# cv1 by one step of Strassen's scheme in six of eight images, its additions in the second attention, and four changes of VectorE's order in attention

## The chip, the cores and the metric

The kernel runs on one core of a Trainium2 chip. What counts is the device time of one execution, in microseconds (us). An execution has five engines that run side by side and wait for each other through semaphores: TensorE (PE in the profile, its weight loads PEld), VectorE (DVE), ScalarE (ACT), GpSimd (POOL) and the sync engine (SP), whose queue issues most of the transfers from and to DRAM. Matmuls write to PSUM, everything else that stays on the core lives in SBUF.

## What is computed

For x of 8 images with 512 channels and 32 x 32 points, all in float32 (`cbs` is convolution, batch norm with fixed statistics, silu):

```python
def layer(x):                                  # called as x + layer(group_norm(x))
    t = cbs(x, cv1_w, cv1_bn, 0)               # 1x1, 512 -> 512 channels
    ys = [t[:, :256], t[:, 256:]]
    for i in range(2):
        yi = ys[-1]
        z = cbs(yi, m_cv1_w[i], m_cv1_bn[i], 1)             # 3x3, 256 -> 256
        z = bot_attention(z, m_qkv_w[i], m_rw[i], m_rh[i])  # 4 heads of 64, 1024 points
        z = silu(bn_eval(conv2d(z, m_cv2_w[i], 0), m_cv2_bn[i]))
        ys.append(yi + z)
    return cbs(concatenate(ys, axis=1), cv2_w, cv2_bn, 0)   # 1x1, 1024 -> 512
```

The attention is softmax(q (k + r) / 8) v with r = rw + rh, for each head over all 1024 points.

## The kernel before

An image is 1024 columns (two halves of 512) by 512 channels (four blocks of 128 partitions). The loop over images is unrolled (`for b in range(B)`, line 1129). For each image: conv3x3 of the first bottleneck (a Winograd form; its transformed input is made by `tiles_in`, line 346, its transformed weights `u` are loaded from DRAM), the first attention, the 1x1 convolution `m2` (line 894), conv3x3 of the second bottleneck, the second attention, `m2`, and cv2. Work of the next image is laid between: cv1 of image b+1 is computed at the end of image b's first attention.

`cv1` (line 857) goes by blocks of 128 output channels: 4 blocks of input channels times 2 halves, 8 matmuls of 128x128 by 512 columns a block, into one PSUM tile of two banks; two silus on ACT take it to y0 (first 256 channels) or into y1, a padded image. Two blocks (y1) are put before and after the last sums of the attention (`first`, `second`, lines 1192 and 1200), two (y0) behind `m2` (line 1214).

cv2 and the q, k, v projection already use one step of Strassen's scheme in Winograd's form (7 products of half-size blocks in place of 8, with four sums of weights and four sums of inputs): `strassen` (line 940), `project_strassen` (line 537). The sums of weights are made once, in image 0 (`make_ws`, `make_sq`), and kept in DRAM.

`attention_fast` (line 637) goes through four groups (channel block c, half), each of four pairs of 128-row tiles. For a pair: `logits` puts 16 matmuls in a PSUM tile for each tile of the pair, ACT takes the exponential (L666), DVE adds it to `acc` (L672 for the first pair of a group, L674 for the others); `times_v` multiplies the pair before by v into `av_ps` (L688), one PSUM tile with a single buffer. When a group is through, ACT copies half of it (L695) and DVE adds the other half (L696), which frees the tile. The sums of a group go over PE (`sums`), to DRAM and back, through a reciprocal (`spread`, L750), and out again as the broadcast tile `rs`; `scale` (L762) multiplies with it. The last group takes a short way (`last_sums`, L724; L796, a reciprocal over 512 elements, L797). What is to be done beside the attention is in the table `behind`: its entry g is called after the first pair of group g, an entry (g, p) after pair p of group g, entries 4 and 5 at the end, before and after `last_sums`.

Order: each engine works through its instructions in a fixed order that the framework's scheduler chooses from priorities (the order in which they are written) and readiness in its own model. `tc.issue_after(ins)` holds the instructions of a block, on the engine of `ins`, behind `ins`. Tiles with one `tag` share its `bufs` buffers: the tag "u" has five buffers of 1 MB for all large weights (u, w1, w2, ws, sq), "x" four, "xr" two, and in PSUM `ps_big` has three tiles of two banks.

Lines that the prediction names: cv1's matmuls L343; the products of cv2's scheme L934; m2's matmuls L900; group norm L443 (bn_stats) and L477 (apply), called step by step from `ahead` through `norm`.

Of the kernel before, what the change touches and what calls it, by code (L numbers as in the profile page):

```python
# [44 lines left out]
F32 = mybir.dt.float32  # L45
I32 = mybir.dt.int32
AF = mybir.ActivationFunctionType
# [14 lines left out]
def kernel(  # L62
# [260 lines left out]
    def stages(act, small, ps_big, ps_av, n_pt):  # L323


        def silu(dst, src, k):

            return nc.scalar.activation(dst, src, AF.Silu, scale=sh[:, k : k + 1], bias=bh[:, k : k + 1])  # L328

        def table_of(func):  # L330

            nc.scalar.activation(spare, zero, func)

        def conv1x1(w_of, rhs_of, nk, ks=None, ps=None, ends=None, by_half=False):

# [201 lines left out]
        def project_strassen(n, z, sq, mid):  # L537
# [35 lines left out]
            def add_r(c, half, src=None):  # L573
                dst = img(kr[:, c, ts(half, HALF)])
                rw = rw_sb[:, n, c, :].unsqueeze(1).to_broadcast([P, ROWS, F])
                rh = rh_sb[:, n, c, ts(half, ROWS)].unsqueeze(2).to_broadcast([P, ROWS, F])
                tt(dst, dst if src is None else img(src), rw, ALU.add)
                tt(dst, dst, rh, ALU.add)

            t = act.tile([P, 4, HALF], F32, tag="pt", name="t_z", bufs=n_pt)  # L580
            t1, t2, t3, t4 = (t[:, i] for i in range(4))
# [55 lines left out]
        def attention_fast(n, z, at, behind, sq=None, mid=None):  # L637
# [13 lines left out]
            def logits(pair):  # L651
                g, j0 = pair[0]
                c, half = groups[g]
                pt = act.tile([P, PAIR, 2, HALF], F32, tag="pt", name="pt", bufs=n_pt)
                pts[pair[0]] = pt
                for i, (_, j) in enumerate(pair):
                    ps = ps_big.tile([P, 2, HALF], F32, tag="big", name="l_ps")
                    for hd in range(2):
                        r = slice(hd * HD, (hd + 1) * HD)
                        for kh in range(2):  # L660
                            o = j * P + kh * HD
                            nc.tensor.matmul(  # L662
                                ps[kh * HD : (kh + 1) * HD, hd, :], kr[r, c, o : o + HD],
                                q[r, c, ts(half, HALF)], start=True, stop=True,
                            )
                    exp = nc.scalar.activation(pt[:, i], ps, AF.Exp, scale=SCALE)  # L666
                if pair is pairs[-1]:
                    with tc.issue_after(exp.ins):
                        table_of(AF.Silu)
                if j0 == 0:  # L670
                    accs[g] = act.tile([P, 2, HALF], F32, tag="acc", name="acc", bufs=2)
                    return nc.vector.tensor_tensor(accs[g], pt[:, 0], pt[:, 1], ALU.add)  # L672
                for i in range(PAIR):
                    ins = nc.vector.tensor_tensor(accs[g], accs[g], pt[:, i], ALU.add)  # L674
                return ins

            def times_v(pair):
                g, j0 = pair[0]
                c, half = groups[g]
                pt = pts.pop(pair[0])  # L680
                if j0 == 0:
                    avs[g] = ps_av.tile([P, 2, HALF], F32, tag="av", name="av_ps")
                for i, (_, j) in enumerate(pair):
                    for kh in range(2):
                        r = slice(kh * HD, (kh + 1) * HD)
                        for hd in range(2):
                            o = c * P + hd * HD
                            nc.tensor.matmul(  # L688
                                avs[g][hd * HD : (hd + 1) * HD, kh, :], vT[r, j, o : o + HD],
                                pt[r, i, hd, :], start=(j == 0), stop=(j == NJ - 1),  # L690
                            )
                if j0 + PAIR == NJ:
                    av = avs.pop(g)
                    dst = ao[:, c, ts(half, HALF)]
                    nc.scalar.copy(dst, av[:, 0])  # L695
                    nc.vector.tensor_tensor(dst, av[:, 1], dst, ALU.add)  # L696

            def sums(g):

# [65 lines left out]


            NQ = NJ // PAIR
            s_drams, rss = {}, {}
# [171 lines left out]
        def strassen(b, ws, y0, y1):  # L940
# [85 lines left out]

            return part1, part2, part3

        def cv2_part(w2, ys, oc, ks=range(2 * NM)):
# [99 lines left out]
    for b in range(B):  # L1129
# [36 lines left out]


        parts = {}


        norm = s.group_norm(xs) if more else iter(())
        groups = iter(range(NM * NH))

        def ahead():
            nonlocal w1
            g = next(groups)
            if g > 0:
                next(norm, None)
            if g == 0:
                w1 = load_w1() if more else load_w2(1)  # L1180
                if b > 0:
                    for at in ((0, 0), (0, 1), (0, 2), (1, 0)):
                        us[at] = load_u(1, *at)
            if b == 0:
                if g == 0:
                    raws[1, 1, 0], raws[1, 1, 1] = load_raws_y0(1, 1)
                    make(1, 1, [2])
                    del us[1, 2]
                elif g <= NM:
                    make(1, 1, [0], [g - 1])  # L1190

        def first():
            nonlocal nxt
# [19 lines left out]
        if more:  # L1213
            s.cv1(w1, xs, nxt, y1n, Y0S)
        else:
            parts[3] = s.cv2_part(w1, (y0, y1), 3)
            parts[0] = s.cv2_part(w1, (y0, y1), 0, range(NM))
# [148 lines left out]
```

## Time and profile before

| | |
|---|---|
| median of 3 runs | 2366.81 us (2366.19 to 2371.23) |
| profiled execution | 2367.23 us, of which the span of its instructions 2365.4 us |
| granted TensorE clock, mean | 0.997 of full speed |
| PE av_ps L688, 4096 records | 487.8 us busy |
| PE l_ps L662, 4096 records | 486.1 us busy |
| PE conv3x3 L879, x u, 2720 records | 306.9 us busy |
| PE cv1, x w, L343, 512 records | 227.1 us busy |
| DVE acc L674, 384 | 469.5 us busy |
| ACT exp L666, 512 | 494.9 us busy |
| transfers | 226.39 MB, mean 96 GB/s |

A float32 matmul appears as two records in the profile. A record's mean time (600 ns for 512 columns) is longer than the distance at which records follow each other, since they are pipelined; the rate is read from how many stand in a stretch. In the tables a group's row ends with the idle time of its engine in front of it and the engine, tile and line that ended most of that time. From one image to the next (images 2 to 6) the same point of the program returns every 288.8 us.

### The profile page before, as it was taken

How to read it: one execution, taken by the hardware profiler on the slowest of the kernel's cores; microseconds unless marked ns; L12 is line 12 of the kernel's file. 1: busy time of each engine (PE TensorE's matmuls, PEld its weight loads, DVE VectorE, ACT ScalarE, POOL GpSimd, SP SyncE). 2: the span in 40 equal slices, each digit the busy share in tenths (PEclk: the TensorE clock that was granted, in tenths of full speed). 3: DMA queues.
4: the chain of work that ended last, by engine and by line, in shares of the span. 5: the costliest groups of instructions: out<-in, count | busy, mean ns of one | idle time of the engine just before them, and what ended most of it. 6: DMA issues, size and time to landing. Idle time of an engine off the chain costs nothing.

```text
span 2365.4 us, 36291 instructions
## 1 busy us (share of the span) xinstructions
PE 2321.6 (98%) x14794; PEld 1181.0 (50%) x14794; DVE 1751.7 (74%) x2811; ACT 944.5 (40%) x1246; POOL 87.9 (4%) x305
## 2 busy tenths in 40 slices
PE   7999999999999999999999999999999999999998
PEld 4536346363553635536364463645536364463643
DVE  8866777677786877868678675886767867677674
ACT  1442524435244351544425344253433525335352
POOL 1000000000100001000010000100001000000001
PEclk9999999999999999999999999999999999999999
DMA  7412225030340304303052031611207021160202
GB/s 251 152 53 89 91 90 213 16 129 15 123 176 15 130 15 164 140 10 130 23 208 89 29 112 33 248 42 54 86 28 263 29 85 55 42 221 15 85 10 69
DMA packets 93069, 226.39 MB, mean 96 GB/s; under 512 B 27872, under 2 KB 49312, under 8 KB 80224
## 3 DMA queue, kind: packets, MB, share of 16 engines
q1 hardware_dynamic: 81376, 174.71, 21.8%
q0 software_dynamic: 11520, 49.29, 5.3%
q8 instruction: 118, 1.93, 0.3%
q14 instruction: 55, 0.45, 0.1%
HBM read 190.41 MB, written 33.55 MB: 95 GB/s over the span
## 4 chain that ended last, share of the span: by engine, by line
PE 89%; DVE 6%; DMA 2%; ACT 2%; issue 1%; SPq 0%; POOL 0%; DVEq 0%; ACTq 0%
PE av_ps L688 16%; PE l_ps L662 15%; PE c_ps L879 14%; PE ps L343 12%; PE c L934 8%; PE p_ps L556 7%; PE c_new L934 6%; PE m_ps L900 5%; PE pv_ps L560 3%; DVE acc L674 2%; ACT pt L666 1%; PE p_ps L560 1%; DVE acc L672 1%; PE s_ps L724 1%; DMA rs<-r_dram 1%; PE s_ps L706 1%
## 5 line engine op out<-in xcount | busy, mean ns | idle before, releaser
L666 ACT ACTIVATE pt<-l_ps 128x1024 f32<-128x1024 f32 x512 | 494.9, 1023 | 425.0 <-PE l_ps L662 423.6
L674 DVE TENSOR_TENSOR acc<-acc,pt 128x1024 f32<-128x1024 f32 x384 | 469.5, 1223 | 84.9 <-ACT pt L666 60.1
L688 PE MATMUL av_ps<-pt,vT 64*64 64x512 f32 x4096 | 487.8, 593 | 10.7 <-DVE ao L696 10.7
L662 PE MATMUL l_ps<-q,kr 64*64 64x512 f32 x4096 | 486.1, 591 | 0.9
L879 PEld LDWEIGHTS c_ps<-v_in,u 128*128 128x128 f32 x2720 | 306.3, 192 | 7.9 <-issue 6.7
L879 PE MATMUL c_ps<-v_in,u 128*128 128x128 f32 x2720 | 306.9, 275 | 1.1 <-DVE v_in L400 1.1
L688 PEld LDWEIGHTS av_ps<-pt,vT 64*64 64x64 f32 x4096 | 157.1, 133 | 284.0 <-issue 216.7
L662 PEld LDWEIGHTS l_ps<-q,kr 64*64 64x64 f32 x4096 | 158.2, 133 | 269.6 <-issue 255.4
L343 PE MATMUL ps<-x,w 128*128 128x512 f32 x512 | 227.1, 600 | 2.2 <-DVE x L477 2.2
L343 PEld LDWEIGHTS ps<-x,w 128*128 128x128 f32 x512 | 97.0, 192 | 130.3 <-issue 127.2
L407 ACT COPY m<-c_ps 128x256 f32<-128x256 f32 x96 | 35.4, 369 | 224.9 <-PE c_ps L879 219.8
L934 PE MATMUL c_new<-t_in,ws 128*128 128x512 f32 x288 | 124.6, 592 | 0.0
L672 DVE TENSOR_TENSOR acc<-pt 128x1024 f32<-128x1024 f32 x64 | 78.3, 1223 | 58.0 <-ACT pt L666 58.0
L900 PE MATMUL m_ps<-ao,m_sb 128*128 128x512 f32 x256 | 112.5, 592 | 0.0
L762 DVE TENSOR_TENSOR ao<-ao,rs 128x512 f32<-128x512 f32 x64 | 44.1, 689 | 65.8 <-DMA rs<-r_dram 65.1
L328 ACT ACTIVATE m_kept<-m_kept,bh,sh 128x512 f32<-128x512 f32 x42 | 31.9, 806 | 146.0 <-DVE m_kept L1018 86.3
L934 PEld LDWEIGHTS c_new<-t_in,ws 128*128 128x128 f32 x288 | 54.8, 190 | 68.8 <-issue 66.0
L328 ACT ACTIVATE t<-m_ps,bh,sh 128x512 f32<-128x512 f32 x64 | 48.0, 775 | 83.9 <-PE m_ps L900 82.5
L556 PE MATMUL p_ps<-t_z,sq 128*128 128x512 f32 x168 | 81.3, 593 | 0.0
L372 POOL MEMSET w_rows<- 128x16 f32 x96 | 12.2, 127 | 1805.6 <-PE s_ps L706 1111.8
L900 PEld LDWEIGHTS m_ps<-ao,m_sb 128*128 128x128 f32 x256 | 48.7, 190 | 61.2 <-issue 61.2
L328 ACT ACTIVATE z<-z,bh,sh 128x512 f32<-128x512 f32 x64 | 48.6, 806 | 50.9 <-DVE z L436 50.9
(223 smaller groups left out, 2704.9 us busy)
## 6 DMA issues: line engine op xcount, KB each, us to landing
u<-u SPq DMA_DIRECT2D x85, 1024.0 KB
x<-in_x_dram SPq DMA_DIRECT2D x32, 512.0 KB
x_res<-in_x_dram POOLq DMA_DIRECT2D x28, 512.0 KB, 8.1
out_dram<-m_kept POOLq DMA_DIRECT2D x28, 512.0 KB, 7.5
w<-in_cv_w_dram SPq DMA_DIRECT2D x13, 1024.0 KB
u<-u_new POOLq DMA_DIRECT2D x12, 1024.0 KB, 5.8
rs<-r_dram SPq DMA_DIRECT2D x96, 128.0 KB
ws<-s SPq DMA_DIRECT2D x24, 512.0 KB
```

Source lines behind the costliest of these rows:

```text
L328: return nc.scalar.activation(dst, src, AF.Silu, scale=sh[:, k : k + 1], bias=bh[:, k : k + 1])
L343: nc.tensor.matmul(ps[:, half, :], w_of(k), rhs_of(k, half), start=(k == begin), stop=(k == end))
L556: nc.tensor.matmul(ps[:, o, :], w[:, o, :], rhs, start=not onto, stop=True, skip_group_check=onto)
L560: nc.tensor.matmul(v[:, ts(j, P)], rhs[:, ts(j, P)], w[:, 2, :], start=j == 0 and not onto, stop=True, skip_group_check=True,)
L662: nc.tensor.matmul(ps[kh * HD : (kh + 1) * HD, hd, :], kr[r, c, o : o + HD], q[r, c, ts(half, HALF)], start=True, stop=True,)
L666: exp = nc.scalar.activation(pt[:, i], ps, AF.Exp, scale=SCALE)
L672: return nc.vector.tensor_tensor(accs[g], pt[:, 0], pt[:, 1], ALU.add)
L674: ins = nc.vector.tensor_tensor(accs[g], accs[g], pt[:, i], ALU.add)
L688: nc.tensor.matmul(avs[g][hd * HD : (hd + 1) * HD, kh, :], vT[r, j, o : o + HD], pt[r, i, hd, :], start=(j == 0), stop=(j == NJ - 1),)
L879: nc.tensor.matmul(ps[:, row, col, :], us[i][:, k, row, SLOT[col], :], vs[i][:, k, row, col, :], start=(k == 0), stop=(k == NM - 1),)
L900: nc.tensor.matmul(pss[oc][:, half, :], m2_sb[:, n, k, ts(oc, P)], ao[:, k, ts(half, HALF)], start=(k == 0), stop=(k == NM - 1),)
L934: nc.tensor.matmul(ps[:, o, :], w[:, k, ts(o, P)], rhs[part][:, c, :], start=(k == 0 and not onto), stop=(k == KB - 1), skip_group_check=onto,
```

## The change

A new function `strassen_cv1` computes cv1 of images 2 to 7 (during images 1 to 6). Its weight sums are made in image 0's second attention (`make_sw`) and loaded with w1 (`load_sw`). Before the last sums of the first attention stand two products and eight additions of 128x512 for t1 to t4 (`begin`), after them a third product onto the first one's PSUM tile and its two silus (`go_on`), behind `m2` the other four (`rest`). Results wait unfinished in y0, y1 and spare tiles; six additions of 128x1024 in the second attention (`add_y0`, `add_y1`) and six silus at its end (`finish`) complete them.

In attention: add_r of the second half in the projection goes ahead of v and q; where the projection is `project_strassen`, the first addition to acc of group 1 is held behind L696; `scale` of a group goes one pair later; in image 0 the steps of the group norm begin one group earlier and make_sq moves. The loads of u for the second conv3x3 go ahead of w1, and the one for its second half of output channels, `load_u(1, 1, 0)`, is no longer made ahead.

```diff
+    sw_dram = tc.dram_tile([P, 4, NX // 2, C], F32, name="sw")
+
+    def make_sw():
+        halves = []
+        for o in range(2):
+            a = act.tile([P, NX, C], F32, tag="x", name="w1_half", bufs=NX)
+            nc.sync.dma_start(a, cv1_w[:, ts(o, C)].rearrange("(k p) o -> p k o", p=P))
+            halves.append((a[:, : NX // 2], a[:, NX // 2 :]))
+        (a11, a12), (a21, a22) = halves
+        parts = [act.tile([P, 2, NX // 2, C], F32, tag="xr", name="sw_new", bufs=2) for _ in range(2)]
+        s1, s2, s3, s4 = (t[:, j] for t in parts for j in range(2))
+        nc.vector.tensor_tensor(s1, a21, a22, ALU.add)
+        nc.vector.tensor_tensor(s2, s1, a11, ALU.subtract)
+        nc.vector.tensor_tensor(s3, a11, a21, ALU.subtract)
+        nc.vector.tensor_tensor(s4, a12, s2, ALU.subtract)
+        for h, t in enumerate(parts):
+            nc.gpsimd.dma_start(sw_dram[:, 2 * h : 2 * h + 2], t)
+
+    def load_sw():
+        w = ring([P, 4, NX // 2, C], "sw")
+        nc.sync.dma_start(w, sw_dram)
+        return w
...
             with tc.issue_after(last.ins):
                 tt(k1, k1, u[:, 1], ALU.add)
-                add_r(0, 1)
+                last = add_r(0, 1)
+            with tc.issue_after(last.ins):
                 tt(v1, v1, v_of(u[:, 2]), ALU.add)
                 tt(q1, q1, u[:, 0], ALU.add)
...
                     with tc.issue_after(exp.ins):
-                        table_of(AF.Silu)
+                        silu_in.append(table_of(AF.Silu))
+                if j0 == 0 and g == 1 and later is not None:
+                    accs[g] = None
+                    return exp
+                return add_up(pair)
+
+            def add_up(pair):
+                g, j0 = pair[0]
+                pt = pts[pair[0]]
                 if j0 == 0:
                     accs[g] = act.tile([P, 2, HALF], F32, tag="acc", name="acc", bufs=2)
                     return nc.vector.tensor_tensor(accs[g], pt[:, 0], pt[:, 1], ALU.add)
...
-                        if at_q == 0 and g > 1:
+                        if at_q == 1 and g > 1:
                             scale(g - 2, rss.pop(g - 2))
...
                     times_v(pairs[i - 1])
+                    if i < len(pairs) and accs.get(pairs[i][0][0], 0) is None:
+                        with tc.issue_after(evicted[0].ins):
+                            added = add_up(pairs[i])
...
+        def strassen_cv1(w, sw, xts, y0, y1):
+            s1, s2, s3, s4 = (sw[:, i] for i in range(4))
+            a11, a12, a22 = (w[:, ts(i, 2), ts(o, C)] for o, i in ((0, 0), (0, 1), (1, 1)))
+            b11, b12, b21, b22 = (
+                [xts[2 * i + c][:, ts(half, HALF)] for c in range(2)] for i in range(2) for half in range(NH)
+            )
...
+            def product(w, rhs, ps=None):
+                onto = ps is not None
+                if not onto:
+                    ps = ps_big.tile([P, 2, HALF], F32, tag="big", name="x_ps")
+                for o in range(2):
+                    for c in range(2):
+                        nc.tensor.matmul(
+                            ps[:, o, :], w[:, c, ts(o, P)], rhs[c], start=(c == 0 and not onto), stop=(c == 1),
+                            skip_group_check=onto,
+                        )
+                return ps
...
+            def begin():
+                t = [act.tile([P, 2, NM, HALF], F32, tag=tag, name="t_x") for tag in ("q", "k")]
+                kept["t"] = t1, t2, t3, t4 = [t[i][:, j] for i in range(2) for j in range(2)]
+                for c in range(2):
+                    tt(t1[:, c], b12[c], b11[c], ALU.subtract)
+                    tt(t2[:, c], b22[c], t1[:, c], ALU.subtract)
+                    tt(t3[:, c], b22[c], b12[c], ALU.subtract)
+                    tt(t4[:, c], t2[:, c], b21[c], ALU.subtract)
+                kept["ps"] = product(a11, b11)
+                kept["m1"] = to(spare("xr", 2), kept["ps"])
+                to(y0_2, product(s4, b22))
+
+            def go_on():
+                ps = product(a12, b21, kept["ps"])
+                for oc in range(NM):
+                    silu(y0[:, oc, ts(0, HALF)], ps[:, oc, :], bn_cv1 + oc)
+
+            def rest():
+                t1, t2, t3, t4 = ([t[:, c] for c in range(2)] for t in kept["t"])
+                kept["m5"] = to(spare("xr", 2), product(s1, t1))
+                kept["m6"] = to(spare("x", NX), product(s2, t2))
+                to(y1_2, product(s3, t3))
+                to(y1_1, product(a22, t4))
+
+            def add_y0():
+                tt(kept["m1"], kept["m6"], kept["m1"], ALU.add)
+                tt(y0_2, y0_2, kept["m1"], ALU.add)
+                tt(y0_2, y0_2, kept["m5"], ALU.add)
+
+            def add_y1():
+                tt(y1_2, y1_2, kept["m1"], ALU.add)
+                tt(y1_1, y1_2, y1_1, ALU.subtract)
+                tt(y1_2, y1_2, kept["m5"], ALU.add)
+
+            def finish():
+                with tc.issue_after(silu_in[-1].ins):
+                    for dst, bn in ((y1_1, bn_cv1 + NM), (y1_2, bn_cv1 + NM), (y0_2, bn_cv1)):
+                        for oc in range(NM):
+                            silu(dst[:, oc, :], dst[:, oc, :], bn + oc)
...
-            if g > 0:
+            if g > 0 or b == 0:
                 next(norm, None)
             if g == 0:
+                if b > 0:
+                    for i in range(PAIRS):
+                        us[0, i] = load_u(1, 0, i)
                 w1 = load_w1() if more else load_w2(1)
-                if b > 0:
-                    for at in ((0, 0), (0, 1), (0, 2), (1, 0)):
-                        us[at] = load_u(1, *at)
+                if more and b > 0:
+                    sw = load_sw()
...
+            if more and b > 0:
+                six = s.strassen_cv1(w1, sw, xs, nxt, y1n)
+                six[0]()
+            elif more:
                 s.cv1(w1, xs, nxt, y1n, Y1S[: NM // 2])
...
-        behind[NG - 2, 2] = lambda: next(norm, None)
-        if b == 0:
+        if b > 0:
+            behind[NG - 2, 2] = lambda: next(norm, None)
+        else:
             behind[-1] = lambda: make(1, 0, range(PAIRS))
...
         last = s.m2(0, ao, y1, lambda oc, half: inner(y2, oc, half))
-        if more:
+        if six:
+            six[2]()
+        elif more:
             s.cv1(w1, xs, nxt, y1n, Y0S)
...
         def first():
+            if six:
+                six[5]()
             if more:
                 three[0]()
...
         if b == 0:
-            behind |= {0: prepare, 2: lambda: make_sq(0), 3: lambda: make_sq(1)}
+            behind |= {0: prepare, 2: lambda: make_sq(0), (2, 2): lambda: make_sq(1), 3: make_sw}
+        if six:
+            behind |= {(1, 1): six[3], (2, 1): six[4]}
```

More of the change, by code (lines that the diff above doesn't have):

```diff
@@ L328, in silu @@
             return nc.scalar.activation(dst, src, AF.Silu, scale=sh[:, k : k + 1], bias=bh[:, k : k + 1])
+        silu_in = []
         def table_of(func):
-            nc.scalar.activation(spare, zero, func)
+            return nc.scalar.activation(spare, zero, func)
         def conv1x1(w_of, rhs_of, nk, ks=None, ps=None, ends=None, by_half=False):
@@ L577, in add_r @@
                 tt(dst, dst if src is None else img(src), rw, ALU.add)
-                tt(dst, dst, rh, ALU.add)
+                return tt(dst, dst, rh, ALU.add)
             t = act.tile([P, 4, HALF], F32, tag="pt", name="t_z", bufs=n_pt)
@@ L695, in times_v @@
                     nc.scalar.copy(dst, av[:, 0])
-                    nc.vector.tensor_tensor(dst, av[:, 1], dst, ALU.add)
+                    evicted[0] = nc.vector.tensor_tensor(dst, av[:, 1], dst, ALU.add)
             def sums(g):
@@ L767, in attention_fast @@
             NQ = NJ // PAIR
-            s_drams, rss = {}, {}
+            s_drams, rss, evicted = {}, {}, [None]
             for i in range(len(pairs) + 1):
@@ L1027, in strassen, with spare, to @@
             return part1, part2, part3
+        def strassen_cv1(w, sw, xts, y0, y1):
[4 more added lines that the diff above has]
+            )
+            tt = nc.vector.tensor_tensor
+            kept = {}
+            def product(w, rhs, ps=None):
[9 more added lines that the diff above has]
+                return ps
+            def spare(tag, bufs):
+                return act.tile([P, 2, HALF], F32, tag=tag, name="x_kept", bufs=bufs)
+            def to(dst, ps):
+                nc.scalar.copy(dst, ps)
+                return dst
+            y0_2, y1_1, y1_2 = side(y0, 1), side(y1, 0), side(y1, 1)
+            def begin():
[32 more added lines that the diff above has]
+                            silu(dst[:, oc, :], dst[:, oc, :], bn + oc)
+            return begin, go_on, rest, add_y0, add_y1, finish
@@ L1168 @@
         parts = {}
+        sw = six = None
         norm = s.group_norm(xs) if more else iter(())
@@ L1174, in ahead @@
         def ahead():
-            nonlocal w1
+            nonlocal w1, sw
             g = next(groups)
-            if g > 0:
+            if g > 0 or b == 0:
                 next(norm, None)
             if g == 0:
+                if b > 0:
+                    for i in range(PAIRS):
+                        us[0, i] = load_u(1, 0, i)
                 w1 = load_w1() if more else load_w2(1)
-                if b > 0:
-                    for at in ((0, 0), (0, 1), (0, 2), (1, 0)):
-                        us[at] = load_u(1, *at)
+                if more and b > 0:
+                    sw = load_sw()
             if b == 0:
@@ L1192, in first @@
         def first():
-            nonlocal nxt
+            nonlocal nxt, six
             if more:
                 nxt = new_y0()
+            if more and b > 0:
+                six = s.strassen_cv1(w1, sw, xs, nxt, y1n)
+                six[0]()
+            elif more:
                 s.cv1(w1, xs, nxt, y1n, Y1S[: NM // 2])
@@ L1200, in second @@
         def second():
-            if more:
+            if six:
+                six[1]()
+            elif more:
                 s.cv1(w1, xs, nxt, y1n, Y1S[NM // 2 :])
@@ L1212 @@
         last = s.m2(0, ao, y1, lambda oc, half: inner(y2, oc, half))
-        if more:
+        if six:
+            six[2]()
+        elif more:
             s.cv1(w1, xs, nxt, y1n, Y0S)
@@ L1258 @@
         if b == 0:
-            behind |= {0: prepare, 2: lambda: make_sq(0), 3: lambda: make_sq(1)}
+            behind |= {0: prepare, 2: lambda: make_sq(0), (2, 2): lambda: make_sq(1), 3: make_sw}
+        if six:
+            behind |= {(1, 1): six[3], (2, 1): six[4]}
         ao, check = s.attention_fast(1, z, (b * N + 1) * NM * NH, behind, sq.get(1), mid)
```

## The prediction

> **What bounds the kernel now.** The head of the page and its chain of waits:
>
> ```profile
> span 2365.4 us, 36291 instructions
> ...
> PE 2321.6 (98%) x14794; PEld 1181.0 (50%) x14794; DVE 1751.7 (74%) x2811; ACT 944.5 (40%) x1246; POOL 87.9 (4%) x305
> ...
> PE 89%; DVE 6%; DMA 2%; ACT 2%; issue 1%; SPq 0%; POOL 0%; DVEq 0%; ACTq 0%
> ```
>
> TensorE (PE) works 98% of the span and carries 89% of the chain, so a matmul removed is time removed, unless another engine fails to keep up. Next, the list of who waited for whom on PE, and the groups by line:
>
> ```profile
> PE av_ps L688 <- DVE ao L696: 10.7, 20, 3.9
> ```
>
> ```profile
> L343 PE MATMUL ps<-x,w 128*128 128x512 f32 x512 | 227.1, 600 | 2.2 <-DVE x L477 2.2
> ...
> L934 PE MATMUL c_new<-t_in,ws 128*128 128x512 f32 x288 | 124.6, 592 | 0.0
> ```
>
> L343 is cv1: 8 images x 32 matmuls, each shown as two records. The first row is the only wait inside the image loop that adds up: `ps_av` has one buffer, and a group's first av matmul waits until VectorE (DVE) has moved the group before out of it. Third, the timeline of image 4 where its first attention ends, the place that is rebuilt, PE's rows and DVE's (start, duration, engine, line, tiles; in brackets the idle time before):
>
> ```profile
> 1319.64 7.13 PE L343 MATMUL ps<-x,w 128*128 128x512 f32 x16
> 1326.70 1.09 PE L724 MATMUL s_ps<-acc,ones 64*64 64x512 f32 x8
> 1327.72 7.13 PE L343 MATMUL ps<-x,w 128*128 128x512 f32 x16
> 1334.69 7.03 PE L900 MATMUL m_ps<-ao,m_sb 128*128 128x512 f32 x16
> ```
>
> ```profile
> 1322.98 0.69 DVE L762 TENSOR_TENSOR ao<-ao,rs 128x512 f32<-128x512 f32 x1 [3.88 <-DMA rs<-r_dram]
> 1323.59 1.22 DVE L674 TENSOR_TENSOR acc<-acc,pt 128x1024 f32<-128x1024 f32 x1
> 1324.72 0.69 DVE L696 TENSOR_TENSOR ao<-av_ps,ao 128x512 f32<-128x512 f32 x1
> 1329.25 0.69 DVE L796 TENSOR_TENSOR rs<-s_ps,s_row 128x512 f32<-128x512 f32 x1 [3.84 <-ACT s_row L731]
> 1329.98 3.35 DVE L797 RECIPROCAL rs<-rs 128x512 f32<-128x512 f32 x1
> 1333.37 0.69 DVE L762 TENSOR_TENSOR ao<-ao,rs 128x512 f32<-128x512 f32 x1
> ```
>
> PE runs without a gap: two cv1 blocks of 7.1 us hide DVE's chain sum, reciprocal, scale, which m2 (L900) reads. One record starts each 0.43 us.
>
> **Part 1: the products.** Plain cv1 is 64 records an image, Strassen's seven products are 7 x 8 = 56. L934's products, of the same shape and order, also take 0.43 us a record (32 in 13.9 us). 8 x 0.43 = 3.44 us an image, six images: **-20.6 us**.
>
> **Part 2: the handover in front of m2.** DVE gets eight additions of 128x512 (t1 to t4, two channel blocks), queued after the last acc. In the trace independent additions of that form start 0.60 us apart (image 4's L613 to L621) though each takes 0.69: 8 x 0.605 = 4.85 us. The Trainium skill ("VectorE: DVE Perf Modes", The DRAIN you can't avoid) says instead that the next operation cannot start until the pipe is empty, so a chain costs full durations: 8 x 0.69 = 5.5 us. New order, from the rows above: last acc ends 1324.8, L696 to 1325.4, additions to 1330.2 by the row (1330.9 by the rule), L796 to 1330.9, reciprocal 3.35 to 1334.3, scale to 1335.0 (1335.7). PE: two products to 1326.7, sums to 1327.7, the one product of `go_on` to 1331.2, and m2 starts 3.5 us earlier than now. It reads the scaled last group only in its second half, after 10 of 16 records, at 1331.2 + 4.3 = 1335.5. So 0.5 us is left by the row and 0.2 us is missing by the rule; I take the row. But scale of group 1 moves to the pair in which x is normalised, which can put everything behind it 0.6 us later. And m2 wants two PSUM buffers of three, while `go_on`'s holds on until its two silus end (1331.2 + 1.5). The other two are free in time (s_ps after L796 at 1330.9, needed at 1332.9), and at the end of the second attention the kernel already takes free buffers past a held one. Were the held one taken first, m2 waits 1.6 us. I take 0.5 us an image, **+3.0 us** (0 to 9.6).
> The four products of `rest` (14 us) stand where cv1's last 13.9 us stood, so tiles_in, ready 5.0, 3.4 and 2.4 us before its three uses now, keeps its cover. ScalarE (ACT) gains six copies of 1.01 us and loses none of its silus (6 of 0.81 us move behind the second attention); between 1320 and 1356 it is busy some 11 of 36 us, and at the second end it idles 6.45 us before the copy at 1460: nothing.
>
> **Part 3: the additions in the second attention.** Three of 128x1024 behind pair 6 and three behind pair 10, each chain 3 x 1.25 = 3.75 us (acc chains start 1.25 to 1.28 apart). What stands behind them on DVE is acc of pairs 7 and 8 and L696, for which PE waits. DVE there now (PE's next av products start at 1428.05):
>
> ```profile
> 1420.95 2.56 DVE L674 TENSOR_TENSOR acc<-acc,pt 128x1024 f32<-128x1024 f32 x2 [0.77 <-ACT pt L666]
> 1425.30 1.23 DVE L672 TENSOR_TENSOR acc<-pt 128x1024 f32<-128x1024 f32 x1 [1.79 <-ACT pt L666]
> 1426.44 0.68 DVE L762 TENSOR_TENSOR ao<-ao,rs 128x512 f32<-128x512 f32 x1
> 1427.05 0.68 DVE L696 TENSOR_TENSOR ao<-av_ps,ao 128x512 f32<-128x512 f32 x1
> ```
>
> Additions 1420.1 to 1423.85, acc of pair 7 to 1426.35 (the sums at 1427.48 still find it), L672 to 1427.5, and, with the scale L762 moved one pair later, L696 to 1428.15: 0.1 us late. The same at pair 10: 1434.7, 1438.4, 1440.9, 1442.05, 1442.7 against 1442.5. Idle 0.77 + 1.79 us and the moved 0.6 us pay nearly all. 0.25 us an image, **+1.5 us** (0 to 12, if each costs 1 us).
>
> **Part 4: DVE's orders.** (a) Where the first pair's acc of group 1 stands behind L696, 14 waits of 0.15 us on L696 go (each about 413.07, 547.36 and so on): **-2.1**. (b) The scale that waits for the rs transfer no longer stands before L696. It caused the waits of 0.82, 0.60 and 0.75 us (716.64, 732.25, 1582.81): **-2.2**, and in image 0 those of 1.86 and 3.89 us:
>
> ```profile
> 146.54 0.69 DVE L762 TENSOR_TENSOR ao<-ao,rs 128x512 f32<-128x512 f32 x1 [3.38 <-DMA rs<-r_dram]
> ```
>
> ```profile
> 147.89 3.39 PE L688 MATMUL av_ps<-pt,vT 64*64 64x512 f32 x16 [3.89 <-DVE ao L696]
> ```
>
> The 16 records after it take 3.39 us, elsewhere 1.95: 1.44 us more. By the Trainium skill ("TensorE: Matmul & The Clock Gate", Part 1) an idle window of about 3.4 us halves PE's clock; the row fits that. By waits alone image 0 holds 5.75 us, with the clock 7.2. Late next there is DVE itself: bn_stats (2.9 us) starts one group earlier, beside make (2.3 us); its 3.96 + 0.99 us of idle in group 0 are too few, and L696 is 1.1 us late there and about as much in group 1. Net **-5.0** (-2 to -7.2). (c) kr before v and q in the projection: no wait stands there; 0. (d) make_sq beside make_sq and make_sw (4 x 0.6 us) in image 0's second attention fill idle time of 1.8 us a group: within 0.5 us.
>
> **Part 5: transfers.** SP's queue is passed by sw (1 MB an image) and the four u loads and w1 in another order. u, w1 and sw take ring buffers that come free at the same places as before (sw that of sq, which SP already waited for until 1258), long before 1319. u(1,0) is no longer prefetched: loaded at conv3x3's second half, needed 10.8 us into it. It can take the buffer of sw or w1 (free at its start), at worst that of the first u, free after 3.6 us. The u loads there issue at 1355.49 and 1359.1 and their packets end about 4 us later: 8 of 10.8 us. sq, behind it, lands some 18 us in, needed after 24. 0.
>
> **Sum** against the profiled execution (span 2365.4, time 2367.23; the runs' median 2366.81 is 0.4 below): -20.6 + 3.0 + 1.5 - 2.1 - 2.2 - 5.0 = -25.4, so 2341.8; as a median **2342 us**.
>
> **Rivals.** About 4.7 us (0.2%) is what a measurement of this kernel can tell from no change.
> 1. The handover binds: m2 waits for the held PSUM buffer or for the scale, 1.6 us an image: -25.4 + 6 x 1.1 gives 2349. For: margins of 0.5 us; against: two free buffers.
> 2. DVE binds in the second attention, each of the 12 additions' places costs 1 us or more: 2342 + 10.5 = 2353; with rival 1 as well 2359. For: 74% busy, no slack left by my sum; against: it fits on paper.
> 3. Slower: u(1,0) gets the buffer of the third u, free only 10.8 us into conv3x3. Landing 4.2 us later, every conv3x3(1) from image 1 on waits 4.4 us, and, past the 3.4 us of the rule above, runs on for a while at half clock, 1.4 us: 7 x 5.8 = 41 us, 2382. It decides from 25.4/7 = 3.6 us a wait on. For: the prefetch is really given up; against: three buffers come free earlier.
> 4. The six images don't get the products, or the orders change nothing: 2363 or 2367. The branch `more and b > 0` is true for six, so unlikely.
>
> **How the numbers follow.** Forecast 0.55 (2335 to 2347), rival 1 0.18, rival 2 0.11, rival 3 and its like (a wait over 4 us an image) 0.11, rival 4 0.05. Low end: all gains, no stall: -20.6 - 7.2 - 2.1 - 2.2 gives 2335. High end: rivals 1 and 2, less their sum: 2356. Faster: 0.55 + 0.18 + 0.10 = 0.83; same 0.06; slower 0.11.
>
> **What would show it.** L343's x rows fall from 512 to 128 records, 336 new ones of 0.43 us stand beside them; m2 follows `go_on` without idle (right) or with 1 to 2 us (rival 1); the row L688 <- L696 falls from 10.7 to about 5 us, without 3.9 as its longest (right) or rises over 12 (rival 2); conv3x3 has no wait on a u transfer (rival 3). DVE's busy time rises by about 6 x 12.9 = 77 us. I am wrong if the period of images 2 to 6, 288.8 us now, does not fall to 285 to 286.5.

## The result and the profile after

The changed kernel takes 2339.26 us (median of 4 runs, 2338.78 to 2339.91) against 2367.14 us before: ratio 0.9876, 95% interval 0.9862 to 0.9891. That is 27.9 us less; 24.8 were forecast. The head of its page and its groups by line, in the same columns as before (lines have moved: L688 is now L723, L662 L689, L696 L731, L762 L797, L674 L709, L900 L938, L934 L972, cv1's L343 is L369 where it is plain and L1084 where it is Strassen's):

```profile
span 2337.2 us, 36365 instructions
...
PE 2298.2 (98%) x14746; PEld 1162.6 (50%) x14746; DVE 1826.2 (78%) x2899; ACT 980.2 (42%) x1282; POOL 88.9 (4%) x307
```

```profile
L369 PE MATMUL ps<-x,w 128*128 128x512 f32 x128 | 58.3, 615 | 2.2 <-DVE x L503 2.2
```

PE has 48 records less (6 x 8), 128 of plain cv1 are left, and DVE works 74.5 us more (77 were forecast). The list of who waited for whom on PE now has two rows that were not there, and the row that was the largest inside the image loop has shrunk (columns: waiter, releaser, us, times, longest):

```profile
PE s_ps L759 <- DVE acc L709: 5.1, 1, 5.1
...
PE c L972 <- DVE ao L731: 1.9, 1, 1.9
...
PE av_ps L723 <- DVE ao L731: 1.1, 2, 0.6
```

The wait of the av products for the eviction (the addition that frees their PSUM tile) fell from 10.7 to 1.1 us; the two new waits happen once each, in image 0. Both traces cut at the same matmuls show where the time came from (us, start to start):

| stretch | before | after | change |
|---|---|---|---|
| image 0: first conv3x3 to first m2 | 128.93 | 121.85 | -7.1 |
| image 0: second conv3x3 to its m2 | 117.65 | 127.60 | **+9.95** |
| images 1 to 6: first conv3x3 to m2, where no rs was late | 113.69 | 109.74 | -3.95 each |
| the same where rs was late, two images | 115.24, 114.50 | 109.74 | 2.4 more |
| images 1 to 7: second conv3x3 to m2, and image 7's first | 112.74 (the last 110.64) | 112.22 (the last 110.12) | -0.51 each |
| m2 to the next conv3x3, images 0 to 6 | 20.60, 41.20 | 20.60, 41.20 (once each 20.66, 20.76) | 0 |

In images 1 to 6 the first attention gains 3.44 us for 8 records and 0.51 us for the orders, and nothing is given back: the handover in front of m2 shows no idle time, nor do the second attentions. The rest of image 0, and a gain of 1 us at the program's two ends, make up the sum of -28.2 us of span. From image 2 to 6 the same point of the program returns every 283.8 us, where it was 288.8.

PE and DVE at the handover of image 4 (start, duration, engine, line, operation):

```profile
1306.89 3.70 PE L1084 MATMUL x_ps<-x,w 128*128 128x512 f32 x8
1310.42 3.60 PE L1084 MATMUL x_ps<-x,sw 128*128 128x512 f32 x8
1313.95 1.09 PE L759 MATMUL s_ps<-acc,ones 64*64 64x512 f32 x8
1314.97 3.70 PE L1084 MATMUL x_ps<-x,w 128*128 128x512 f32 x8
1318.51 7.03 PE L938 MATMUL m_ps<-ao,m_sb 128*128 128x512 f32 x16
```

```profile
1316.49 0.69 DVE L1106 TENSOR_TENSOR t_x<-t_x,x 128x512 f32<-128x512 f32 x1
1317.10 0.69 DVE L731 TENSOR_TENSOR ao<-av_ps,ao 128x512 f32<-128x512 f32 x1
1317.69 0.68 DVE L834 TENSOR_TENSOR rs<-s_ps,s_row 128x512 f32<-128x512 f32 x1
1318.41 3.35 DVE L835 RECIPROCAL rs<-rs 128x512 f32<-128x512 f32 x1
1321.80 0.69 DVE L797 TENSOR_TENSOR ao<-ao,rs 128x512 f32<-128x512 f32 x1
```

The eight additions (the last is the first row of DVE) follow each other 0.60 us apart; the scale ends at 1322.49. m2 reads it with its eleventh record, at 1318.51 + 10 x 0.43 = 1322.8, 0.3 us later.

And the new loss, image 0's second attention (columns as before, in brackets the idle time and what ended it):

```profile
286.20 0.69 DVE L246 TENSOR_TENSOR sw_new<-w_half 128x512 f32<-128x512 f32 x1 [2.55 <-DMA w_half<-in_cv_w_dram]
...
291.39 1.23 DVE L709 TENSOR_TENSOR acc<-acc,pt 128x1024 f32<-128x1024 f32 x1
301.46 0.69 DVE L797 TENSOR_TENSOR ao<-ao,rs 128x512 f32<-128x512 f32 x1 [8.84 <-DMA rs<-r_dram]
302.07 1.22 DVE L709 TENSOR_TENSOR acc<-acc,pt 128x1024 f32<-128x1024 f32 x1
```

```profile
303.43 1.98 PE L759 MATMUL s_ps<-acc,ones 64*64 64x512 f32 x8 [5.11 <-DVE acc L709]
307.35 9.00 PE L972 MATMUL c<-t_in,s 128*128 128x512 f32 x16 [1.93 <-DVE ao L731]
```

DVE's order has a scale between the two last additions to acc. That scale waits 8.84 us for its rs transfer; acc, the sums on PE and, by L731, the product that wants `ps_av` wait behind it. Before the change the same scale waited 4.02 us, and no instruction of PE waited for it:

```profile
300.67 0.69 DVE L762 TENSOR_TENSOR ao<-ao,rs 128x512 f32<-128x512 f32 x1 [4.02 <-DMA rs<-r_dram]
```

After 5.11 us of idle PE runs at half clock (last section): s_ps takes 1.98 us in place of 1.09 and 16 records 9.00 in place of 7.13. 5.1 + 1.9 + 0.9 + 1.9 = 9.8 us.

### The profile page after: what moved, and what is told of

Same layout as the page of the kernel before. It is cut to its first block, busy times and chain, and to the rows that moved or that the text cites. A ratio compares the mean times of both kernels' runs of the same rounds, so it can differ in the third digit from the quotient of the medians.

```text
span 2337.2 us, 36365 instructions
## 1 busy us (share of the span) xinstructions
PE 2298.2 (98%) x14746; PEld 1162.6 (50%) x14746; DVE 1826.2 (78%) x2899; ACT 980.2 (42%) x1282; POOL 88.9 (4%) x307
## 3 DMA queue, kind: packets, MB, share of 16 engines
q8 instruction: 118, 1.93, 0.3%
## 4 chain that ended last, share of the span: by engine, by line
PE 93%; DVE 4%; DMA 1%; ACT 1%; issue 0%; SPq 0%; POOL 0%; DVEq 0%; ACTq 0%
PE av_ps L723 18%; PE l_ps L689 18%; PE c_ps L917 14%; PE c L972 8%; PE p_ps L582 7%; PE x_ps L1084 6%; PE c_new L972 6%; PE m_ps L938 5%; PE ps L369 5%; PE pv_ps L586 3%; PE s_ps L741 1%; PE p_ps L586 1%; DVE acc L709 1%; PE s_ps L759 1%; PE v_ps L553 1%
## 5 line engine op out<-in xcount | busy, mean ns | idle before, releaser
L709 DVE TENSOR_TENSOR acc<-acc,pt 128x1024 f32<-128x1024 f32 x384 | 469.4, 1222 | 65.8 <-ACT pt L693 42.5
L723 PE MATMUL av_ps<-pt,vT 64*64 64x512 f32 x4096 | 485.1, 591 | 1.1 <-DVE ao L731 1.1
L689 PE MATMUL l_ps<-q,kr 64*64 64x512 f32 x4096 | 484.2, 590 | 0.0
L723 PEld LDWEIGHTS av_ps<-pt,vT 64*64 64x64 f32 x4096 | 152.0, 133 | 277.3 <-issue 230.7
L689 PEld LDWEIGHTS l_ps<-q,kr 64*64 64x64 f32 x4096 | 153.7, 133 | 269.7 <-issue 256.2
L972 PE MATMUL c_new<-t_in,ws 128*128 128x512 f32 x288 | 124.6, 592 | 0.0
L938 PE MATMUL m_ps<-ao,m_sb 128*128 128x512 f32 x256 | 112.7, 593 | 0.0
L797 DVE TENSOR_TENSOR ao<-ao,rs 128x512 f32<-128x512 f32 x64 | 44.1, 689 | 60.4 <-DMA rs<-r_dram 59.8
L972 PEld LDWEIGHTS c_new<-t_in,ws 128*128 128x128 f32 x288 | 54.7, 190 | 68.9 <-issue 66.0
L938 PEld LDWEIGHTS m_ps<-ao,m_sb 128*128 128x128 f32 x256 | 48.4, 190 | 61.7 <-issue 58.4
L946 DVE TENSOR_TENSOR ylast<-t,ypad 128x512 f32<-128x512 f32 x32 | 22.0, 692 | 66.5 <-ACT t L352 66.5
L426 DVE TENSOR_TENSOR v_in<-w_rows 128x512 f32<-128x512 f32 x96 | 65.9, 687 | 0.0
L972 PE MATMUL c<-ypad,ws 128*128 128x512 f32 x144 | 63.8, 592 | 0.0
```

Of the source, the lines that this page charges most:

```text
L689: nc.tensor.matmul(ps[kh * HD : (kh + 1) * HD, hd, :], kr[r, c, o : o + HD], q[r, c, ts(half, HALF)], start=True, stop=True,)
L723: nc.tensor.matmul(avs[g][hd * HD : (hd + 1) * HD, kh, :], vT[r, j, o : o + HD], pt[r, i, hd, :], start=(j == 0), stop=(j == NJ - 1),)
L938: nc.tensor.matmul(pss[oc][:, half, :], m2_sb[:, n, k, ts(oc, P)], ao[:, k, ts(half, HALF)], start=(k == 0), stop=(k == NM - 1),)
L972: nc.tensor.matmul(ps[:, o, :], w[:, k, ts(o, P)], rhs[part][:, c, :], start=(k == 0 and not onto), stop=(k == KB - 1), skip_group_check=onto,
```

## The experiments

All times are medians of 4 or 5 runs, each kernel beside runs of the kernel before on its chip. They were taken in three sets: experiments 1, 2, 3 and 6; then 5, 7, 8 and 9; then 4, 10 and the two repetitions. The changed kernel took 2339.26 us when it was first measured and 2337.61 us in the last set, so a difference between sets can be off by some 1.5 us or more, and the traces decide where it matters.

**1. The orders alone.** Plain cv1 everywhere, no sums of cv1's weights:

```diff
-            if more and b > 0:
-                six = s.strassen_cv1(w1, sw, xs, nxt, y1n)
-                six[0]()
-            elif more:
+            if more:
...
-                if more and b > 0:
-                    sw = load_sw()
...
-            behind |= {0: prepare, 2: lambda: make_sq(0), (2, 2): lambda: make_sq(1), 3: make_sw}
+            behind |= {0: prepare, 2: lambda: make_sq(0), (2, 2): lambda: make_sq(1)}
```

> The changed kernel with plain cv1 in all images, without make_sw and load_sw: VectorE's orders alone, the result is the same. Theory (read from the stretches of the two traces): the orders are worth 14 x 0.51 us in the attentions whose projection is Strassen's, 7.1 us in image 0's first attention and 2.2 us of late rs transfers, 16.4 us together: 2350.7. Rival (the sum as predicted): 2.1 + 2.2 + 5.0 = 9.3 us, 2357.8, and the six images gain more than 20.6 us from the products.

Measured: 2348.72 us (2347.17 to 2350.41), 18.2 below the kernel before, ratio 0.9923 (0.991 to 0.9937). The theory holds, the rival falls. The new order of the loads of u is still in this run, beside DVE's orders. Against the changed kernel's trace its six first attentions are 3.43 or 3.44 us longer each (20.6 in all), image 0's second attention is 9.8 us shorter, and image 0's first 1.6 us (the clock, last section). So some 60% of the measured gain, 16.6 us without the clock's 1.6, are the orders'. Strassen's products net only 9.5 us: image 0's second attention gives 9.8 of their 20.6 back, and the clock's 1.6 us stand between the two kernels as well.

**2. Without the add_r order.**

```diff
-                last = add_r(0, 1)
-            with tc.issue_after(last.ins):
+                add_r(0, 1)
                 tt(v1, v1, v_of(u[:, 2]), ALU.add)
```

> The changed kernel with add_r of the second half not held in front of v and q. Theory: kr's second half reached PE late by about 0.24 to 0.36 us in each of 14 attentions, a wait too short to show as idle time, so this order is worth 3.4 to 5.0 us: 2342.7 to 2344.3. Rival (as predicted): worth nothing, 2339.3.

Measured: 2340.19 us (2339.93 to 2341.09), 0.9 above the changed kernel of another set; by the trace each of the 14 attentions is 0.28 us longer. It was repeated beside the changed kernel.

> The run with add_r not held, once more. By its trace each of 14 attentions is 0.28 us longer, 3.9 us together, while its median was only 0.9 us over that of the changed kernel, taken in another call. Theory: 3.9 us over the changed kernel in this call. Rival: 1 us or less, the trace's difference is made up elsewhere.

Measured: 2341.84 against 2337.61 us, 4.2 more: 14 x 0.28 = 3.9. The theory holds; the comparison across two sets had been off by 3 us. (In the two profiles image 0 differs as well, by -1.6 us, the clock, in its first attention and +1.1 us in its second.)

**3. Without the acc order of group 1.**

```diff
-                if j0 == 0 and g == 1 and later is not None:
-                    accs[g] = None
-                    return exp
```

> The changed kernel with the first acc of group 1 in front of L731 (L696 before) again. Theory: 14 waits of 0.15 us shown, 0.22 us by start to start: 2.1 to 3.1 us slower, 2341.4 to 2342.4. Rival: the earlier kr has already removed them, 2339.3.

Measured: 2348.69 us (2347.61 to 2349.18), 9.4 above the changed kernel of another set: three times what the theory said, and the rival is wrong too. By the trace it is 0.76 us in each of 14 attentions, 10.6 together. The end of image 4's group 0 in this kernel:

```profile
1267.44 1.90 PE L689 MATMUL l_ps<-q,kr 64*64 64x512 f32 x16
1269.27 0.64 PE L738 MATMUL s_ps<-acc,ones 128*32 128x256 f32 x8
1270.60 1.95 PE L720 MATMUL av_ps<-pt,vT 64*64 64x512 f32 x16 [0.69 <-DVE ao L728]
```

```profile
1268.72 1.22 DVE L704 TENSOR_TENSOR acc<-pt 128x1024 f32<-128x1024 f32 x1
1269.86 0.68 DVE L728 TENSOR_TENSOR ao<-av_ps,ao 128x512 f32<-128x512 f32 x1
```

In group 0 DVE does not idle; it is the limit there. With kr earlier PE reaches the group's end sooner and then waits longer for the eviction (L728, the L731 of the changed kernel), 0.69 us where it was 0.15. The two orders should then hang together, and undoing both should cost less than undoing this one.

**4. Both undone.** Edits 2 and 3 together.

> The changed kernel with both the add_r order and the acc order of group 1 as before. Theory (the two hang together: an earlier kr lets PE reach the end of group 0 sooner, where it then waits for L731 unless that stands in front of acc): 14 x 0.51 us = 7.1 us slower than the changed kernel, and so faster than the run in which only the acc order is undone, 14 x 0.76 = 10.6 us. Rival (two separate gains): slower than either undone alone, 14 x (0.28 + 0.76) = 14.6 us.

Measured: 2345.56 us (2343.21 to 2346.36), 7.95 above the changed kernel of the same set (2337.61) and 3.1 below run 3; by the trace 0.51 us in each of 14 attentions. The theory holds: the earlier kr is worth 0.28 us beside the other order and costs 0.25 us without it. That PE arrives sooner explains why nothing is gained there, but not a cost. The cost is on DVE. In run 3 three steps that need each other's result stand in a row:

```profile
1254.14 0.69 DVE L652 TENSOR_TENSOR kr<-kr,u_z 128x512 f32<-128x512 f32 x1
1254.86 0.69 DVE L603 TENSOR_TENSOR kr<-kr,rw_sb 128x512 f32<-128x512 f32 x1
1255.59 0.69 DVE L604 TENSOR_TENSOR kr<-kr,rh_sb 128x512 f32<-128x512 f32 x1
```

They start 0.72 and 0.73 us apart. With both orders undone a step of v or q stands between them and all start 0.60 us apart. Twice 0.12 us is the 0.25 us by which DVE, the limit of group 0, reaches the eviction later in run 3.

**5. Without the moved scale.**

```diff
-                        if at_q == 1 and g > 1:
+                        if at_q == 0 and g > 1:
```

> The changed kernel with scale(g - 2) at the first pair of a group again. Theory: the moved scale pays for the additions in the second attention; without it L731 is late by 0.6 us or more at 12 places (7.3 us), image 0 loses 7.1 us and late rs transfers 2.2 us: 2356. Rival: only the late transfers return, 2348.6; the additions are hidden anyway.

Measured: 2349.24 us (2347.51 to 2351.75), 10 above the changed kernel of another set: near the rival's number, but not for its reason. In its trace (the slowest of the five, 13.0 us above that of the changed kernel) av waits for L731 22 times, 16.3 us:

```profile
PE av_ps L723 <- DVE ao L731: 16.3, 22, 2.0
```

The second attentions of images 1 to 6 are 1.3 to 2.5 us longer each, so the moved scale does pay for the additions there, 0.5 us at the first place and 0.7 to 1.8 at the second; the first attentions of these images are 0.4 to 2.6 us longer. The sum is less than forecast for two reasons. Image 0's first attention lost 3.7 us and not 7.1. And its second came out 4.8 us shorter (there make_sw did not wait for its loads, and rs landed earlier against PE's work); runs 6 to 8 take up that place.

**6. The loss in image 0: order on DVE.**

```diff
-            scale(g - 1, rss.pop(g - 1))
+            with tc.issue_after(added.ins):
+                scale(g - 1, rss.pop(g - 1))
```

> The changed kernel with the last scale(g - 1) of an attention held behind the last acc on VectorE. Theory A (order): in image 0's second attention the 7.0 us that PE waits, and the slow records after it, 10 us together, come from acc standing behind a scale whose rs transfer is late; they go: 2329.3. Rival B (VectorE's work itself, the w_half wait of 2.55 us and the sums of 2.5 us, makes acc late): at most half goes, 2334 or more. The other 13 attentions had 0.4 us or more to spare there and change by less than 1 us in all.

Measured: 2334.60 us (2332.57 to 2335.65), half of what theory A said. That is the number of rival B, but not its cause: the sums no longer wait for acc at all. The product behind them now waits 4.07 us, and its 16 records then take 8.83 us in place of 7.13:

```profile
301.13 0.69 DVE L797 TENSOR_TENSOR ao<-ao,rs 128x512 f32<-128x512 f32 x1 [4.37 <-DMA rs<-r_dram]
...
302.88 0.68 DVE L731 TENSOR_TENSOR ao<-av_ps,ao 128x512 f32<-128x512 f32 x1
```

L731 still stands behind the scale. The chain was right, its second half had been left out: the late transfer, not acc alone, has to be dealt with. In the other attentions nothing changes by more than 0.04 us.

**7. The loss in image 0: transfers.** The sums of weights in tiles of other tags, so that x_res need not wait for their stores:

```diff
-        parts = [act.tile([P, 2, NX // 2, C], F32, tag="xr", name="sw_new", bufs=2) for _ in range(2)]
-        s1, s2, s3, s4 = (t[:, j] for t in parts for j in range(2))
+        parts = [act.tile([P, NX // 2, C], F32, tag=tag, name="sw_new", bufs=2) for tag in ("wt", "wt", "t", "t")]
+        s1, s2, s3, s4 = parts
...
-            nc.gpsimd.dma_start(sw_dram[:, 2 * h : 2 * h + 2], t)
+            nc.gpsimd.dma_start(sw_dram[:, h], t)
```

> The changed kernel with make_sw's sums in tiles of tags wt and t in place of xr, so that the two x_res loads of image 0 need not wait for the stores of the sums. Theory B (crowded transfers): x_res and the u load no longer stand in front of the rs transfer, its wait on VectorE falls from 8.84 to about 4 us as before the change and the 10 us go: 2329.3. Rival: rs is late because its chain starts late (reciprocal at 291.2), the wait falls by 2 us or less: 2337 or more.

Measured: 2334.23 us (2332.30 to 2334.83). The wait fell from 8.84 to 4.39 us, as said, but the time by 5 us and not by 10: 1.2 us at the sums and 2.8 at the product are left, and 1.7 us of slow records behind them (8.83 us for 16). The scale still stands in front of acc and L731, and its chain still starts late: the reciprocal of the sums (L785, L750 before) starts 103.1 us after the start of conv3x3 in this run, 102.6 in the changed kernel, 98.8 in the kernel before. The rival is right in that. The u load that the theory names is issued behind rs (298.35 against 294.73), so it did not stand in front of it. The edit also makes four stores of the two; the run doesn't separate that from the tiles.

**8. Both.** Edits 6 and 7.

> Both: the last scale behind the last acc, and sums in tiles of their own. If either alone removes the stall, this equals it, 2329.3; if each removes a part, it is the only one at 2329.3.

Measured: 2328.25 us (2327.57 to 2329.18), ratio to the kernel before 0.9831 (0.9818 to 0.9845). Each edit removes a part, and both are needed: image 0's second attention is 4.1 us shorter with either alone, 9.35 with both. The scale now stands behind acc and waits 1.02 us:

```profile
296.57 0.69 DVE L797 TENSOR_TENSOR ao<-ao,rs 128x512 f32<-128x512 f32 x1 [1.02 <-DMA rs<-r_dram]
```

One idle gap of 0.54 us is left at that place. The transfers tell the rest. Issues of x_res by POOL in the changed kernel, and then in this one (start, duration, tile; in brackets what POOL waited for):

```profile
292.33 0.73 POOL L1016 DMA_DIRECT2D x_res<-in_x_dram  x1 [2.68 <-DMA sw<-sw_new]
294.83 0.74 POOL L1016 DMA_DIRECT2D x_res<-in_x_dram  x1 [1.76 <-DMA sw<-sw_new]
```

```profile
244.88 1.46 POOL L1017 DMA_DIRECT2D x_res<-in_x_dram  x2
```

In the changed kernel rs, issued by SP at 294.73, lands 6.7 us later, beside x_res; with x_res out of the way, nearly 50 us earlier, rs is issued at 293.12 and lands in 3.4. Two issuing engines share the transfer engines, as the Trainium skill says ("DMA: Bandwidth & Descriptors", Issuing engines are not separate DMA queues).

> The run with the last scale behind the last acc and sums in tiles of their own, once more: 11 us under the changed kernel in this call, 2328.3.

Measured: 2328.24 us (2328.04 to 2328.39), 9.4 below the changed kernel of the same set and not 11, ratio to the kernel before 0.9836 (0.9822 to 0.9849). In the two profiles image 0's second attention is 9.4 us shorter; its first is 1.6 us shorter too (the clock), and the first conv3x3 begins 0.8 us later. This version beats both kernels.

**9. More additions in front of m2.**

```diff
                     tt(t4[:, c], t2[:, c], b21[c], ALU.subtract)
+                    tt(t4[:, c], t2[:, c], b21[c], ALU.subtract)
+                    tt(t4[:, c], t2[:, c], b21[c], ALU.subtract)
```

> The changed kernel with t4 computed three times over in begin: four additions of 128x512 more in each of six images. Theory: in front of m2 VectorE has 0.36 us to spare (scale ends 1322.49, m2's eleventh record reads it at 1322.85); four more cost 2.4 us, so m2 waits 2.05 us, six times: 12.3 us, 2351.6. Rival: VectorE has more to spare there, 2345 or less.

Measured: 2351.80 us (2350.65 to 2353.12); 2351.6 were expected, a closer match than the working deserves. The waits appear at the two places that the prediction names, the PSUM tile of the sums and the scaled group:

```profile
PE m_ps L938 <- DVE ao L797: 7.6, 6, 1.3
PE m_ps L938 <- DVE rs L834: 4.7, 6, 0.9
```

The waits shown are 2.05 us an image, but from start to start m2 takes 2.5 to 2.7 us longer, some 15 us in six images: a wait loses part of its length to the modelled end of the record in front of it, and the second record behind a wait starts 0.53 us after the first in place of 0.43. DVE's delay is 2.7 us and not 2.4, since the repeated t4 start 0.72 us apart in part. The median hides this, since it is set against the changed kernel of another set. The rival falls either way, and the handover has about 0.3 us to spare. In the changed kernel m2 starts at 1318.51, while the silus that free `go_on`'s PSUM buffer end at 1320.16: m2 did take free buffers past the held one.

**10. The changed kernel again.**

> The changed kernel once more, unchanged, beside the others of this call: 2339.3. It is what the undone orders are compared with on the same chip.

Measured: 2337.61 us (2336.90 to 2338.28). Its trace has the same stretches within 0.2 us; the medians of the two sets differ by some 1.6 us.

## Why the prediction was right, and where it was off

The forecast 2342 and its range hold the 2339.3, but errors of both signs met, and that they nearly cancelled is luck. Images 1 to 7 were to gain 20.4 us and gained 30.1; image 0 was to gain 5.0 and lost 2.9; 1.1 us more came at the program's two ends. The prediction's own sign shows it: the period of images 2 to 6 was to fall to 285 to 286.5 us and fell to 283.8, so the account of the repeated part was too careful. (The sum itself gives 2366.81 - 25.4 = 2341.4 as a median; 2342 is nearer to the profiled execution.)

| step of the sum | forecast | measured | by |
|---|---|---|---|
| products, six images | -20.6 | -20.6 | run 1 |
| handover in front of m2 | +3.0 | 0, 0.3 us to spare | trace, run 9 |
| additions in the second attention | +1.5 | 0, paid by the moved scale | runs 1 and 5 |
| acc order (a), and kr's order (c) | -2.1, 0 | -7.1 together | runs 2 to 4 |
| late rs, images 1 to 7 | -2.2 | -2.4 | trace |
| image 0, first attention | -5.0 | -7.1 | trace |
| image 0, second attention (d) | 0 to 0.5 | **+9.95** | runs 6 to 8 |

- The products were sized right to 0.01 us an image, and the timing of the handover as well: scale was said to end 0.5 us ahead of its use, it ends 0.3 ahead. Of the two prices for the additions the row (0.60 us apart) was right, not the 0.69 that the rule gave; the section of the Trainium skill that it cites ("VectorE: DVE Perf Modes", The DRAIN you can't avoid) also says that an operation which is not held starts earlier, and the prediction left that out. The +3.0 us were an allowance for what could not be seen, and the additions' +1.5 an estimate of 0.1 us of lateness that did not occur: three of them take 3.6 us and not 3.75, from the start of the first to the acc behind them. (The acc additions start 1.33 us apart, not 1.25 to 1.28; the prediction's own row has two in 2.56 us. Its sum did not depend on that.) Of the rivals, the late u load never appeared: in image 4 the first of the u loads issued 3 us before conv3x3 began, and no product waited for one.
- Order (c) was costed at nothing because "no wait stands there". There was one. In image 4's second attention of the kernel before, the third pair's logits started 1.96 us after the products in front of them, elsewhere 1.72:

```profile
1398.66 1.90 PE L688 MATMUL av_ps<-pt,vT 64*64 64x512 f32 x16
1400.62 1.95 PE L662 MATMUL l_ps<-q,kr 64*64 64x512 f32 x16
```

As the end of such a block is modelled 1.90 us after its start, only 0.06 us of idle showed. The 0.15 us of each of the 14 waits of (a) was 0.22 for the same reason.

- Image 0's first attention gained 7.1 us where 5.0 were taken as the net. Run 5 gives 3.7 of it back without the moved scale; how the rest is shared among the other orders, no run separates.
- Step (d) failed: within 0.5 us was said, +9.95 measured. It costed make_sw as 4 x 0.6 us of DVE that "fill idle time". Its DMAs were left out: the loads of w_half, for which DVE waits 2.55 us in order, the stores, and x_res, which had to wait for buffers of "xr" that the sums now held and so came to stand beside the rs transfer. The row that would have warned was in the profile of before: the scale of that attention already waited 4.02 us for rs in front of the last acc, and those of the other attentions 2.9 to 4.9.

## What to carry to other kernels

When a step is put into a crowded place, count what it holds as well as what it computes: a buffer tag that it takes can push another engine's transfer onto a third one's deadline. Where an engine keeps a fixed order, an instruction that waits for a transfer must not stand in front of one that frees a PSUM tile or feeds the busiest engine; look for such pairs even where they cost nothing yet. And for pipelined matmuls measure waits from start to start, since a wait shorter than the modelled tail shows as little or no idle time.

## What the runs showed of the hardware

The clock of PE reacts to idle time in a way that a list of waits doesn't show. The granted clock in stretches of the changed kernel (columns: stretch, length, busy time and instructions of PE, PEld, DVE, ACT, POOL, clock, share of DMA, GB/s):

```profile
303.00:309.00 6.00, 3.63 (x10) 1.17 (x11) 5.96 (x7) 1.07 (x2) 0.17 (x2) 0.50 0.00 1
308.00:317.00 9.00, 9.00 (x18) 3.79 (x17) 3.97 (x2) 0.61 (x1) 0.00 (x0) 0.83 0.02 1
```

After the wait of 5.11 us, which ends at 303.43, PE ran at half clock until 311, through a second wait of 1.93 us: 0.83 over the 9 us from 308 is half clock for 3 of them. That is some 8 us, and it added 2.8 us to the 7.0 of waiting. No single wait has to be as long as the 3.4 us that the prediction took from the skill's rule, here the measurement decides: in run 7 waits of 1.2 and 2.8 us were followed by slow records as well (16 in 8.83 us in place of 7.13). A quieter case: image 0's first conv3x3 has two waits of 1.3 and 1.2 us, and in some executions the clock of that stretch is 0.93, in others 1.00 (before and after 0.93, run 8 1.00). That makes 1.6 us between profiles in the same stretch of the program, which a comparison of a few microseconds has to take out. What decides between the two is not shown.
